# Seven products for queries and keys, PSUM sums and byte masks in a two-layer graph network on one core

## The chip, the cores and the metric

The kernel runs on one core of one Trainium2 chip. The metric is the time of one execution on the device in microseconds (us), here the median over runs.

## The reference

There are 64 graphs of 256 nodes with 256 features (x is 64x256x256, float32) and an adjacency matrix adj (64x256x256, int32, entries 0 or 1, the diagonal set). Each graph passes through two layers. Cut to what matters:

```python
# layer 0: two graph attentions, a norm, a feed-forward block with relu, a norm
def gat(h, W, a):
    Wh = h @ W
    e = leaky_relu(Wh @ a[:256] + swap(Wh @ a[256:]), 0.2)
    return softmax(where(adj > 0, e, -9e15), axis=1) @ Wh
h = norm(x + gat(gat(x, W1, a1), W2, a2), g_ln1, b_ln1)
x = norm(h + relu(h @ w_ff1 + b_ff1) @ w_ff2 + b_ff2, g_ln2, b_ln2)
# layer 1: attention of 8 heads of 32, one value projection for each relation r
q, k = x @ Wq + bq, x @ Wk + bk
attn = softmax(q @ k.T / sqrt(32))
out = sum((attn * (adj == r)) @ (x @ Wv[r] + bv[r]) for r in range(4))
y = norm(x + out @ Wo + bo, g1, beta1)
y = norm(y + gelu(y @ W1 + b1) @ W2 + b2, g2, beta2)
```

## The kernel before

Everything is float32. A graph's 256x256 arrays lie in SBUF as two tiles of 128 partitions. The function `binary` handles adjacency of zeros and ones, for which only relations 0 and 1 occur; a second function, for other adjacency, stands behind a branch that the given data do not take.

The work of a graph is cut into named pieces. `G.` is graph attention up to the first norm, `F.` the first feed-forward block with its norm and then queries and keys, `A.` the attention of layer 1, `T.` the output projection, the second feed-forward block and the last norm, `L.` the loads, `S.` the preparation of weights. Three written lists give the order: `START`, then `PERIOD` for each period, then `END`. An entry `F.q/2` in `PERIOD` runs piece `F.q` for the graph that entered two periods ago, so that six graphs are under way at once. Every engine (PE, DVE, ACT, POOL, and SP, whose queue issues the transfers) executes its own instructions in the order of the lists, and waits at the head of its queue when something it needs is not there. With lags of up to 5 there are 59 full periods.

The pieces that the change and the prediction speak of, and their lines in the code before:

- `G.wh`, `G.wc` project x with the joint weights wx (L751, L761). `G.e` spreads one column of scores into a PSUM tile (L767), `G.lr` adds the other on ACT into the SBUF tile s (L775), `G.ad` on DVE applies the leaky slope (L780), the mask `away` (L781) and takes the maximum (L783), and `G.ex` on ACT takes the exponentials (L788). `G.rz` scales by the inverse sums (L798). `G.gA` and `G.gB` multiply on PE (L804).
- A norm (`ln`, `rs`, `nm`): `ln` on DVE adds the residual to the PSUM result and writes an SBUF tile acc (L506), and takes statistics (L511 to L514); `rs` on POOL takes the root (L518); `nm` on DVE writes the normalised y (L523). `ra`, `rb` on POOL weight y for the next residual (L558, L565). Three norms of a graph have this form; the last one (`D`) has its own finish (L533, L540).
- Turning: `dt` transposes by a DMA in 16-bit words into a tile `pairs` (L473), `dm` moves it by two DMAs into `halves` (L481), and `c` or `mg` joins the halves into float32 on ACT or POOL (L488). Each head of the attention is turned like this, and each y.
- Seven products: `seven_products` replaces the eight block products of a 2x2 block multiplication by seven, with factors and sums prepared (`s` on POOL, L588). Its PE pieces are `a` to `e`; `k1` to `k4` take a first value out of a PSUM bank and `p1` to `p3` add a bank to it (L641). Both first products of the feed-forward blocks (`h`), the second of layer 1 (`f`) and the values (`v`, L852) use it.
- `F.q` and `F.k` are plain products (L839), of two row blocks by two column blocks, and `F.qe`, `F.ke` take them out on ACT with bias and scale (L849). `A.sc` computes the scores of four heads (L884), `A.mx` their maxima, `A.ex` the exponentials, `A.pm` the part with relation 1 (L949), `A.o` the outputs (L957), `A.oc` scales them, and `T.wo` projects (L974).

All PSUM tiles of the loop have one tag with eight buffers, one for each bank; `mm_tile` takes a buffer that is free:

```python
def mm_tile(name, shape=(P, 2, 256)):
    return psum.tile(list(shape), F32, tag="mm", name=name, bufs=8)
```

The joint weights wx are prepared once at the start (`joint_weights`, L341 to L366): W1 times W2 on PE, and both layers' score vectors multiplied in on DVE.

Of the kernel before, what the change touches and what calls it, by code (L numbers as in the profile page):

```python
# [25 lines left out]
F32 = mybir.dt.float32  # L26
U8 = mybir.dt.uint8
# [7 lines left out]
P = 128  # L35
# [8 lines left out]
A.dm10/4 A.mg10/4 L.xT/0 A.zj/4 T.hp2/5 T.ge0/5 A.pm02/4 T.he/5 F.dmA/1 A.pm10/4 F.lnB/2 A.sc0/3  # L44
A.o0/4 T.raC/5 F.cA/1 A.mx10/3 A.o1/4 A.mx03/3 A.mx00/3 T.ge1/5 F.rsB/2 A.oc0/4 A.mx01/3 T.hk4/5
A.dt13/3 A.dt12/3 F.sA/1 T.rbC/5 G.wh0/0 T.ge2/5 L.adj/0 A.oc1/4 T.ge3/5 A.dm13/3 A.ex00/3
A.dm12/3 A.ex01/3 G.wh1/0 G.wc0/0 G.away/0 A.mg12/3 G.wc1/0 F.ha/1 G.eA/0 F.hb/1 A.dt11/3 T.u0/5
A.mx02/3 A.mg13/3 F.nmB/2 G.lrA/0 F.hk1/1 F.hk2/1 T.wo/4 A.ex03/3 A.dt00/3 G.adA/0 T.lnC/4
A.ex10/3 F.raB/3 G.exA/0 A.dm11/3 T.u1/5 A.dm00/3 T.fb/5 A.mg00/3 F.hc/1 T.fa/5 F.hk3/1 A.mg11/3
F.hd/1 G.rzA/0 A.dt03/3 F.hp3/1 F.dtB/2 A.ex02/3 T.fk1/5 F.hp1/1 G.gA0/0 T.rsC/4 G.gA1/0 G.wd0/0  # L50
T.nmC/4 A.dm03/3 G.wd1/0 T.fk2/5 A.va/3 F.dmB/2 T.fp1/5 A.vk1/3 A.vb/3 F.hp2/1 T.dtC/4 G.eB/0
T.u3/5 G.lrB/0 F.rbB/3 T.fc/5 A.iz/3 F.he/1 F.cB/2 A.mg03/3 A.vk2/3 T.fk3/5 T.u2/5 G.adB/0 F.raA/1
A.vc/3 T.fd/5 A.vp1/3 A.dt01/3 F.r0/1 L.x/0 T.fp2/5 G.exB/0 T.dmC/4 A.pm11/3 F.k/2 A.vk3/3 F.q/2
T.fe/5 F.hk4/1 A.zt/3 G.rzB/0 A.pm00/3 A.dm01/3 F.ke0/2 T.cC/4 F.ke1/2 F.r1/1 A.vd/3 A.vp3/3
F.r2/1 F.qe0/2 F.rbA/1 T.fp3/5 A.dt02/3 T.sC/4 T.fk4/5 A.zd/3 A.dt10/3 T.lnD/5 G.gB/0 F.qe1/2
# [9 lines left out]
L.adj:2 L.adj:1 G.wh0:0 S.lr:0 G.away:0 G.wc0:0 G.wh1:0 G.wc1:0 G.eA:0 G.lrA:0 S.f0:0 S.v0:0  # L65
G.adA:0 G.exA:0 G.rzA:0 G.gA0:0 G.gA1:0 G.wd0:0 G.wd1:0 L.xT:1 G.eB:0 G.lrB:0 S.f1:0 G.adB:0
G.exB:0 G.wh0:1 G.wc0:1 S.q0:0 S.j2:0 G.rzB:0 G.wh1:1 G.gB:0 G.wc1:1 S.v1:0 G.away:1 G.eA:1
G.lnA:0 G.lrA:1 S.lw:0 G.rsA:0 L.x:1 G.nmA:0 G.adA:1 S.l0:0 L.xT:2 G.wh1:2 G.exA:1 S.v2:0 G.wh0:2
G.rzA:1 F.raA:0 F.dtA:0 G.wc0:2 L.adj:3 G.gA1:1 S.f2:0 S.q1:0 F.dmA:0 F.cA:0 G.gA0:1 G.wd0:1
F.sA:0 G.wd1:1 F.ha:0 F.hb:0 G.eB:1 S.l1:0 F.hk1:0 F.hk2:0 G.lrB:1 G.wc1:2 F.hc:0 F.hk3:0 G.adB:1  # L70
F.hp3:0 F.hd:0 F.hp2:0 G.exB:1 G.rzB:1 L.xT:3 F.hp1:0 G.wh1:3 F.he:0 F.r0:0 G.gB:1 F.r1:0 F.hk4:0
S.j1:0 F.r2:0 F.r3:0 G.lnA:1 G.away:2 G.wh0:3 G.rsA:1 G.wc0:3 L.x:2 G.nmA:1 G.eA:2 F.f0:0 F.f1:0
G.lrA:2 G.adA:2 F.dtA:1 G.exA:2 F.dmA:1 F.cA:1 G.wc1:3 F.rbA:0 G.rzA:2 S.v3:0 F.lnB:0 S.w1:0
G.gA1:2 G.gA0:2 F.rsB:0 F.ha:1 F.nmB:0 G.eA:3 G.wd0:2 G.wd1:2 G.eB:2 F.hk1:1 F.sA:1 F.hb:1 F.hk2:1
G.lrB:2 F.hc:1 F.hk3:1 L.xT:4 G.adB:2 F.dtB:0 F.dmB:0 F.cB:0 G.away:3 G.exB:2 F.hd:1 F.q:0 F.hp2:1
S.w2:0 F.qe0:0 G.rzB:2 F.qe1:0 F.k:0 F.hp3:1 G.gB:2 F.r0:1 F.ke0:0 F.ke1:0 F.r1:1 A.sc1:0 F.hp1:1
G.lnA:2 G.lrA:3 A.mx12:0 F.he:1 F.hk4:1 A.sc0:0 A.ex12:0 G.rsA:2 F.r2:1 G.nmA:2 F.r3:1 F.sB:0
A.mx13:0 F.raA:1 A.dt12:0 F.dtA:2 A.mx11:0 A.ex11:0 A.mx03:0 A.ex13:0 A.dm12:0 G.adA:3 A.mx01:0
F.dmA:2 F.f0:1 G.exA:3 A.mx10:0 A.dt13:0 A.mx00:0 G.rzA:3 F.rbA:1 A.mg12:0 F.f1:1 A.ex00:0
A.dt00:0 F.cA:2 G.gA1:3 F.sA:2 F.lnB:1 A.dm13:0 F.ha:2 A.ex03:0 F.hb:2 A.mx02:0 A.dm00:0 G.gA0:3  # L80
F.rsB:1 F.hk1:2 F.hk2:2 A.mg00:0 F.nmB:1 F.dtB:1 F.raB:0 G.wd0:3 G.wd1:3 G.eB:3 A.ex10:0 A.dt11:0
G.lrB:3 A.pm12:0 F.hc:2 G.wh0:4 A.mg13:0 G.wh1:4 A.vb:0 F.hk3:2 F.hp1:2 G.adB:3 F.dmB:1 A.dm11:0
F.hd:2 F.raA:2 A.ex02:0 A.va:0 G.wc0:4 F.cB:1 A.dt03:0 F.hp2:2 A.mg11:0 F.raB:1 F.q:1 G.exB:3
A.dt10:0 F.hp3:2 F.rbA:2 F.he:2 G.rzB:3 F.r0:2 A.vk1:0 G.wc1:4 A.ex01:0 A.vk2:0 F.k:1 A.vc:0
F.ke0:1 L.x:3 F.ke1:1 A.dm03:0 A.vk3:0 A.dm10:0 G.gB:3 A.vp3:0 F.qe0:1 A.iz:0 A.mg10:0 A.mg03:0
G.eA:4 F.qe1:1 F.hk4:2 A.pm13:0 G.lnA:3 A.dt02:0 A.pm00:0 A.dt01:0 A.sc1:1 A.mx12:1 A.mx13:1
F.r1:2 F.r2:2 F.r3:2 A.zt:0 A.dm02:0 G.rsA:3 G.nmA:3 A.dm01:0 A.vd:0 G.lrA:4 A.mx11:1 A.pm03:0
A.zd:0 A.ex12:1 A.mg02:0 F.dtA:3 A.ex11:1 A.vp2:0 A.mg01:0 A.pm11:0 A.vp1:0 A.dt12:1 A.zr:0 F.f0:2
A.pm01:0 A.sc0:1 A.pm02:0 A.pm10:0 A.mx01:1 A.ex13:1 F.f1:2 A.dm12:1 A.ve:0 A.mx02:1 A.mx00:1
A.mx10:1 L.adj:4 A.vk4:0 F.lnB:2 A.ex01:1 F.dmA:3 F.rsB:2 A.o1:0 A.mg12:1 G.away:4 F.cA:3 G.adA:4  # L90
# [1248 lines left out]
```

## Time and profile before

| What | Value |
|---|---|
| Median of 3 runs | 3160.0 us (3155.21 to 3164.05) |
| The profiled execution | 3154.81 us, its span 3153.0 us |
| Mean granted TensorE clock | 0.988 |
| PE, DVE, ACT, POOL busy | 95%, 83%, 77%, 59% of the span |

The busy share of PE counts matmuls that overlap one another once, and a matmul that is issued but waits inside the pipeline as busy. A float32 matmul leaves two MATMUL records and two LDWEIGHTS records. In answers about a line, three durations with slashes are the least, the median and the greatest in ns. In answers about a stretch, each engine's busy time stands with the count of its instructions, in the order PE, weight load, DVE, ACT, POOL, then the granted clock, the share of the DMA engines and GB/s. In answers about waits, the total in us, the times and the longest follow the colon. In a timeline, a line has start, length, engine, code line and operation; in brackets stands the idle time before it and what ended it.

### The profile page before, as it was taken

To read this page: it belongs to the slowest core of one execution; us is meant where nothing else is said; L and a number is where in the kernel's file an instruction comes from. 1 tells how busy PE (TensorE), PEld (TensorE's weight loads), DVE (VectorE), ACT (ScalarE), POOL (GpSimd) and SP (SyncE) were. 2 spreads that over 40 slices of the span, in tenths; PEclk is the share of its full clock that TensorE was granted. 3 is DMA by queue.
4 is the path that set the end of the run, shared out by engine and by line. 5 is a ranking of instruction groups with operands and counts; after the bars stand their busy time and mean duration, and the time that the engine had idled before them with its cause. 6 is when DMAs were issued, how large, how long until landed. Compare 5 with 4: busy or idle time off the path is not lost.

```text
span 3153.0 us, 67189 instructions
## 1 busy us (share of the span) xinstructions
PE 3008.8 (95%) x23274; PEld 2615.6 (83%) x23274; DVE 2627.9 (83%) x5425; ACT 2424.5 (77%) x5632; POOL 1861.0 (59%) x2161
## 2 busy tenths in 40 slices
PE   6899999999999999999999999999999999999986
PEld 5688888888888888888888888888888888888875
DVE  5688888898889898888888888888888988888865
ACT  2677877877877877877877877878877877877863
POOL 4466556656656656656556556656656656656554
PEclk8999999999999999999999999999999999999998
DMA  5577777777777787777887777777787777777763
GB/s 162 114 145 152 155 151 148 158 156 149 154 152 149 154 152 145 156 155 149 151 152 153 152 152 152 152 157 152 152 152 150 155 148 151 153 155 148 145 138 69
DMA packets 1049529, 468.72 MB, mean 149 GB/s; under 512 B 788416, under 2 KB 1039296, under 8 KB 1049184
## 3 DMA queue, kind: packets, MB, share of 16 engines
q1 hardware_dynamic: 1047920, 462.12, 73.7%
q8 instruction: 186, 3.05, 0.5%
q0 software_dynamic: 976, 1.72, 0.3%
q14 instruction: 159, 1.30, 0.2%
q10 hardware_dynamic: 288, 0.52, 0.1%
HBM read 75.65 MB, written 17.30 MB: 29 GB/s over the span
## 4 chain that ended last, share of the span: by engine, by line
PE 53%; DMA 15%; DVE 14%; ACT 7%; POOL 4%; issue 4%; SPq 2%; POOLq 0%; DVEq 0%; ACTq 0%
DMA halves_p<-pairs_p 9%; PE ff_a L690 8%; PE fX_c L706 5%; PE hX_c L665 5%; PE o L957 4%; PE hX_a L665 3%; PE q L839 3%; PE k L839 3%; DVE y_c L523 3%; PE gat_b L804 3%; POOL pm L488 3%; PE sc L884 3%; PE wh L751 2%; DMA pairs_p<-p 2%; PE hY_c L665 2%
## 5 line engine op out<-in xcount | busy, mean ns | idle before, releaser
L488 POOL COPY pm<-halves_p 128x1024 uint16<-128x1024 uint16 x256 | 350.5, 1369 | 551.5 <-DMA halves_p<-pairs_p 518.2
L690 PE MATMUL ff_a<-w_L_gnn_w_ff,hid_a 128*128 128x256 f32 x2048 | 463.2, 379 | 0.3 <-ACT hid_a L682 0.3
L949 DVE TENSOR_TENSOR pm<-pm,adj 128x512 f32<-128x512 f32 x512 | 389.6, 794 | 49.9 <-POOL pm L488 48.4
L690 PEld LDWEIGHTS ff_a<-w_L_gnn_w_ff,hid_a 128*128 128x128 f32 x2048 | 379.5, 190 | 48.0 <-issue 0.7
L488 ACT COPY pm<-halves_p 128x1024 uint16<-128x1024 uint16 x256 | 347.0, 1355 | 9.7 <-DMA halves_p<-pairs_p 9.4
L588 POOL TENSOR_TENSOR S_c<-cols_c 128x128 f32<-128x128 f32 x128 | 58.4, 456 | 416.0 <-ACT cols_c L488 416.0
L957 PE MATMUL o<-pm,v 128*32 128x256 f32 x4096 | 236.7, 381 | 4.3 <-POOL pm L488 1.7
L682 ACT ACTIVATE hid_c<-hid_c,col_L_gnn_b 128x256 f32<-128x256 f32 x512 | 224.5, 498 | 4.9 <-DVE hid_c L641 2.0
L682 ACT ACTIVATE hid_a<-hid_a,col_L_gnn_b_ff 128x256 f32<-128x256 f32 x512 | 223.9, 501 | 0.7 <-DVE hid_a L641 0.6
L957 PEld LDWEIGHTS o<-pm,v 128*32 128x32 f32 x4096 | 126.2, 110 | 104.1 <-issue 21.8
L706 PE MATMUL fX_c<-f_L_gnn_W,hid_c 128*128 128x128 f32 x1536 | 205.0, 276 | 3.3 <-ACT hid_c L682 2.4
L706 PEld LDWEIGHTS fX_c<-f_L_gnn_W,hid_c 128*128 128x128 f32 x1536 | 197.0, 192 | 12.2 <-ACT hid_c L682 3.6
L523 DVE TENSOR_SCALAR y_c<-acc_c,mv_c,rstd_c 128x256 f32<-128x256 f32 x128 | 157.2, 1268 | 34.4 <-POOL rstd_c L518 34.4
L488 ACT COPY cols_a<-halves_y_a 128x1024 uint16<-128x1024 uint16 x64 | 86.4, 1349 | 101.5 <-DMA halves_y_a<-pairs_y_a 101.3
L884 PE MATMUL sc<-kT,qT 32*128 32x256 f32 x2048 | 148.9, 400 | 0.9 <-DVE v L641 0.9
L665 PEld LDWEIGHTS hX_c<-S_c,f_L_gnn_W 128*128 128x128 f32 x1024 | 128.9, 191 | 24.0 <-issue 20.2
L665 PEld LDWEIGHTS hX_c<-cols_c,f_L_gnn_W 128*128 128x128 f32 x1024 | 134.3, 192 | 14.2 <-ACT cols_c L488 4.8
L665 PE MATMUL hX_a<-cols_a,f_L_gnn_w_ff 128*128 128x128 f32 x1024 | 137.6, 277 | 6.0 <-ACT cols_a L488 2.9
L775 ACT ACTIVATE s_B<-e_B,wh_B 128x256 f32<-128x256 f32 x128 | 53.7, 471 | 116.4 <-PE e_B L767 116.4
L852 PE MATMUL vY<-f_Wv,S_y 128*128 128x256 f32 x256 | 84.4, 412 | 61.2 <-DVE acc_c L641 57.9
L665 PEld LDWEIGHTS hX_a<-cols_a,f_L_gnn_w_ff 128*128 128x128 f32 x1024 | 128.6, 192 | 16.8 <-ACT p L899 8.0
L665 PE MATMUL hX_c<-cols_c,f_L_gnn_W 128*128 128x128 f32 x1024 | 136.5, 276 | 5.4 <-ACT cols_c L488 3.6
(1741 smaller groups left out, 9328.8 us busy)
## 6 DMA issues: line engine op xcount, KB each, us to landing
halves_p<-pairs_p SPq DMA_DIRECT2D x1024, 128.0 KB, 3.3
xT<-in_xT SPq DMA_DIRECT2D x64, 256.0 KB, 3.5
adj<-in_adjT SPq DMA_DIRECT2D x64, 256.0 KB, 3.3
x<-in_x SPq DMA_DIRECT2D x64, 256.0 KB, 3.3
halves_y_a<-pairs_y_a SPq DMA_DIRECT2D x128, 128.0 KB, 3.9
halves_y_y<-pairs_y_y SPq DMA_DIRECT2D x128, 128.0 KB, 3.3
zs<-flat SPq DMA_DIRECT2D x256, 64.0 KB, 2.7
halves_y_c<-pairs_y_c SPq DMA_DIRECT2D x128, 128.0 KB, 3.2
```

The lines of the kernel that those rows point to most:

```text
L488: copy(into().bitcast(U16).rearrange("p (n s) -> p s n", s=2), t["halves"].rearrange("p s k q -> p s (k q)"),)
L523: nc.vector.tensor_scalar(y[:, :, :, i, :], tiles["acc"][:, i, :].rearrange("p (k c d) -> p c k d", k=KC, c=2), tiles["mv"][:, i, 0:1], ti ...
L665: nc.tensor.matmul(ps[:, f * P : (f + 1) * P], weights()[0][:, factor, f * P : (f + 1) * P], left, start=start and f == 0, stop=f == FC // ...
L682: nc.scalar.activation(tiles["hid"][:, f, :], tiles["hid"][:, f, :], func, bias=b1[:, f : f + 1])
L690: nc.tensor.matmul(tiles["ff"][:, i, :], tiles["hid"][:, f, nodes(i)], weights()[2][:, f, :], start=(f == 0), stop=(f == FC - 1),)
L706: nc.tensor.matmul(ps, left[:, f, :], weights()[2][:, factor, f * P : (f + 1) * P], start=start and f == 0, stop=f == FC // 2 - 1, skip_gr ...
L804: nc.tensor.matmul(ps, t["s"][:, j, nodes(i)], t["whz"][:, j, :width], start=(j == 0), stop=(j == NT - 1),)
L839: nc.tensor.matmul(t[key + "p"][:, o, :], w[:, c, nodes(o)], tiles["cols"][:, c, :], start=(c == 0), stop=(c == KC - 1),)
L852: nc.tensor.matmul(ps, left, wv[:, factor, :], start=start, stop=True, skip_group_check=True)
L884: nc.tensor.matmul(t["sc", g, hh][:, i, :], qkv["q"][hd, g, nodes(i)], qkv["k"][hd, g, :], start=True, stop=True,)
L949: nc.vector.tensor_tensor(pm[:, 1, :], pm[:, 0, :], tiles["adj"], ALU.mult)
L957: nc.tensor.matmul(ps[hh * DH : (hh + 1) * DH, :], qkv["v"][:, j, d0 : d0 + DH], t["pm", (g, hh)][:, r, j * N : (j + 1) * N], start=(r == ...
```

## The change

1. **Queries and keys.** Wq and Wk become one set of seven factors `wqk`, prepared like those of the values, with the biases in one tile `bqk`; the query half is scaled by 1/sqrt(32) in the preparation. Pieces `F.q`, `F.k`, `F.qe0/1`, `F.ke0/1` go; `F.qa` to `F.qe`, `F.qk1` to `F.qk4` and `F.qp1` to `F.qp3` come. The first values are taken out on DVE with the bias added.
2. **PSUM.** A norm adds the residual in place in the PSUM bank, and statistics and y read the bank. The scores of the graph attention after slope and mask are written to the bank of `e`, and the exponentials read it.
3. **Bytes.** `A.pm` takes the mask as bytes from `away`, which therefore lives as long as the graph's attention (four buffers), while the int32 adjacency has one buffer instead of four.
4. **Buffers.** `pairs` and `halves` have three tiles instead of two, `pm` seven instead of eight.
5. **Joint weights.** The part of W1 comes before that of the product W1 W2; W1 is loaded on ACT's queue; the score sums are written straight into wx.
6. **Orders.** `START`, `PERIOD` and `END` are new throughout.

```diff
-T.nmC/4 A.dm03/3 G.wd1/0 T.fk2/5 A.va/3 F.dmB/2 T.fp1/5 A.vk1/3 A.vb/3 F.hp2/1 T.dtC/4 G.eB/0
+A.ex03/3 F.lnB/2 G.wc0/0 A.oc0/4 F.dmA/1 A.va/3 A.oc1/4 A.ex01/3 G.wh1/0 T.u0/5 A.mg13/3 F.rsB/2
+A.vb/3 G.away/0 A.dt12/3 F.nmB/2 A.vk1/3 G.wc1/0 A.vk2/3 F.raA/1 T.wo/4 T.u1/5 G.eA/0 F.cA/1
...
+F.hp3/1 G.wd0/0 T.fp1/5 F.qa/2 A.pm13/3 T.dmC/4 F.hp2/1 T.u2/5 F.qb/2 T.fc/5 A.zd/3 A.dt00/3
...
+T.fe/5 F.hk4/1 G.adB/0 F.r1/1 F.qe/2 T.fk4/5 G.exB/0 F.qk4/2 T.lnD/5 T.ha/4 T.sC/4 T.hk1/4 F.rbA/1
+T.nmD/5 G.rzB/0 T.hb/4 T.rsD/5 A.sc1/2 A.mx10/2 A.pm03/3 T.hk2/4 A.dm00/3 T.rbC/4 T.hp1/4 A.o1/3
...
-        for a, n in ((a2, "L0_gnn_a2"), (a1, "L0_gnn_a1")):
+        for a, n in ((a1, "L0_gnn_a1"), (a2, "L0_gnn_a2")):
...
-        for w, n in ((w1T, "L0_gnn_W1T"), (w2, "L0_gnn_W2"), (w1, "L0_gnn_W1")):
-            nc.sync.dma_start(out=w, in_=t[n].rearrange("(c p) n -> p c n", p=P))
+        for queue, w, n in (
+            (nc.sync, w1T, "L0_gnn_W1T"), (nc.scalar, w1, "L0_gnn_W1"), (nc.sync, w2, "L0_gnn_W2"),
+        ):
+            queue.dma_start(out=w, in_=t[n].rearrange("(c p) n -> p c n", p=P))
...
-        nc.vector.tensor_copy(wx[:, :, :D], ps)
-        for w, a, at in ((wx, a2, SRC2), (w1, a1, SRC1)):
+        for w, a, at in ((w1, a1, SRC1), (wx, a2, SRC2)):
+            if w is wx:
+                nc.vector.tensor_copy(wx[:, :, :D], ps)
             for c in range(KC):
-                both = small.tile([P, 2], F32, tag="wa", name=f"wa_{at}_{c}", bufs=1)
                 prod = work.tile([P, 2, D], F32, tag="res", name=f"prod_{at}_{c}", bufs=3)
-                nc.vector.tensor_tensor(
-                    prod, a, w[:, c, :D].unsqueeze(1).to_broadcast([P, 2, D]), ALU.mult
-                )
-                nc.vector.tensor_reduce(both, prod, AX.X, ALU.add)
-                nc.vector.tensor_copy(wx[:, c, at : at + 1], both[:, 1:2])
-                nc.vector.tensor_copy(wx[:, c, at + 1 : at + 2], both[:, 0:1])
+                for half in range(2):
+                    nc.vector.tensor_tensor(prod[:, half, :], a[:, 1 - half, :], w[:, c, :D], ALU.mult)
+                nc.vector.tensor_reduce(wx[:, c, at : at + 2], prod, AX.X, ALU.add)
...
-            t["pairs"] = work.tile([P, 2, 4, P], U16, tag="pairs", name=f"pairs_{name}", bufs=2)
+            t["pairs"] = work.tile([P, 2, 4, P], U16, tag="pairs", name=f"pairs_{name}", bufs=3)
...
-            acc, *terms = src()
-            if terms:
-                acc = work.tile([P, NT, D], F32, tag="acc", name=f"acc_{name}", bufs=2)
-                nc.vector.tensor_tensor(acc, *terms, ALU.add)
+            acc, *residual = src()
+            if residual:
+                nc.vector.tensor_tensor(acc, acc, *residual, ALU.add)
...
-            ps = t["e"] = mm_tile(f"e_{step}{b}", (P, N))
+            t["e"] = mm_tile(f"e_{step}{b}", (P, NT, N))
...
-            nc.vector.scalar_tensor_tensor(t["s"], t["s"], ALPHA, t["s"], ALU.mult, ALU.max)
-            nc.vector.scalar_tensor_tensor(t["s"], t["away"], NEG, t["s"], ALU.mult, ALU.add)
+            nc.vector.scalar_tensor_tensor(t["e"], t["s"], ALPHA, t["s"], ALU.mult, ALU.max)
+            away = tiles["away"].rearrange("p (t i) -> p t i", t=NT)
+            nc.vector.scalar_tensor_tensor(t["e"], away, NEG, t["e"], ALU.mult, ALU.add)
...
-        def project(w, key):
-            t[key + "p"] = mm_tile(f"{key}_{b}")
+        def columns(ps, factor, left, start):
             for o in range(KC):
-                for c in range(KC):
-                    nc.tensor.matmul(
-                        t[key + "p"][:, o, :], w[:, c, nodes(o)], tiles["cols"][:, c, :],
-                        start=(c == 0), stop=(c == KC - 1),
-                    )
...
+                nc.tensor.matmul(
+                    ps[:, nodes(o)], wqk[:, factor, nodes(o)], left,
+                    start=start and o == 0, stop=o == KC - 1, skip_group_check=True,
+                )
...
+        def begin_qk(i, h, ps):
+            nc.vector.tensor_tensor(
+                qk(i, h), ps.rearrange("p (o n) -> p o n", n=P),
+                bqk[:, h, :].unsqueeze(2).to_broadcast([P, KC, P]), ALU.add,
+            )
...
+        seven_products(do, "F", "q", b, *by_columns(tiles), columns, begin_qk, qk, D)
...
-            nc.vector.tensor_tensor(pm[:, 1, :], pm[:, 0, :], tiles["adj"], ALU.mult)
+            nc.vector.scalar_tensor_tensor(
+                pm[:, 1, :], tiles["away"], 0.0, pm[:, 0, :], ALU.is_equal, ALU.mult
+            )
```

## The prediction

> **What bounds the kernel now.** I read the busy rows first, then the same counts in four windows far from both ends, then the waits of PE and SP, then a piece of PE's timeline, and last the rows of the DVE lines that the change touches.
>
> ```profile
> PE 3008.8 (95%) x23274; PEld 2615.6 (83%) x23274; DVE 2627.9 (83%) x5425; ACT 2424.5 (77%) x5632; POOL 1861.0 (59%) x2161
> ```
> ```profile
> 540.00:1015.00 475.00, 465.31 (x3651) 406.60 (x3650) 410.60 (x847) 381.30 (x888) 289.27 (x334) 1.00 0.76 153
> sum 1900.00, PE 1855.26 PEld 1621.87 DVE 1632.86 ACT 1520.73 POOL 1149.25; mean PE 463.81 PEld 405.47 DVE 408.21 ACT 380.18 POOL 287.31
> ```
> ```profile
> PE vY L852 <- DVE acc_c L641: 57.9, 57, 1.9
> PE wh L751 <- DVE wx L366: 9.0, 1, 9.0
> SPq L473 <- DMA halves_p<-pairs_p: 343.9, 410, 2.8
> ```
> ```profile
> 1540.07 1.06 PE L665 MATMUL hX_a<-cols_a,f_L_gnn_w_ff 128*128 128x128 f32 x8
> 1540.96 0.60 PE L852 MATMUL vX<-f_Wv,S_y 128*128 128x256 f32 x2
> ...
> 1542.72 1.89 PE L839 MATMUL k<-cols_y,w_L_gnn_Wk 128*128 128x256 f32 x8
> 1544.45 1.89 PE L839 MATMUL q<-cols_y,w_L_gnn_Wq 128*128 128x256 f32 x8
> 1546.18 1.05 PE L706 MATMUL fX_c<-f_L_gnn_W,hid_c 128*128 128x128 f32 x8
> ...
> 1584.98 0.70 PE L852 MATMUL vY<-f_Wv,S_y 128*128 128x256 f32 x2 [1.25 <-DVE acc_c L641]
> ...
> 1587.52 1.06 PE L665 MATMUL hX_a<-cols_a,f_L_gnn_w_ff 128*128 128x128 f32 x8
> ```
> ```profile
> L523 DVE TENSOR_SCALAR y_a<-acc_a,mv_a,rstd_a x128: 402/544/1347, 45.0 to 2972.8; 128x256 f32<-128x256 f32 x128
> L523 DVE TENSOR_SCALAR y_c<-acc_c,mv_c,rstd_c x128: 399/1352/1422, 164.5 to 3114.8; 128x256 f32<-128x256 f32 x128
> L949 DVE TENSOR_TENSOR pm<-pm,adj x512: 628/684/1807, 112.6 to 3103.0; 128x512 f32<-128x512 f32 x171
> L781 DVE SCALAR_TENSOR_TENSOR s_B<-away,s_B x64: 691/1647/1661, 36.6 to 2959.4; 128x512 f32<-128x512 uint8 x64
> L506 DVE TENSOR_TENSOR acc_a<-gat_b,x x64: 686/691/693, 42.0 to 2968.5; 128x512 f32<-128x512 f32 x64
> ```
>
> The same hX_a group starts at 1540.07 and 1587.52: a period is 47.45 us, and 1900 us hold 40 of them. In a period PE is busy 1855.3/40 = 46.4 us and idle 1.1; DVE works 40.8, ACT 38.0, POOL 28.7. PE is the bound. About 1.0 of its 1.1 us of idling is one wait, 57 times in the run: bank Y of the value products waits for a DVE add that empties a bank of the last feed-forward product (`A.vb` stands two entries behind `T.fp1` in the written order). So only two things can shorten the middle: fewer matmul columns, and that wait. Beside it PE idles 353 - 278.8 = 74 us in the first 200 and last 153 us.
>
> **Queries and keys by seven products.** From 1542.72 to 1546.18, k and q take 3.46 us: 16 records of 256 columns, 0.216 each (a matmul leaves two records). The new form has seven products of two matmuls: 28 records of 128 columns. The nearest rows are hX_a and fX_c, also 128x128 by 128 columns, eight per group: 1540.07 to 1540.96 is 0.89, or 0.111 each. 28 x 0.111 = 3.12 us, so -0.34 per graph. Here the Trainium skill speaks against the change: "TensorE: Matmul & The Clock Gate", section "Back-to-back issue gap", gives a sustained 81 ns for a 128-column matmul because its weight load must be paid too. With two passes per record that would be 28 x 0.162 = 4.5 us, +1.1 per graph, +69 us in all. The row has loads and products together at 0.111, so I take the row. A group that really waited starts slower (a vY pair 0.53 after its wait, to 1585.51, against 0.44 at 1540.96); there are now five pieces instead of two, and I allow one such start, +0.11. Net -0.23.
> Off PE: ACT loses four evictions of 0.465, -1.9 us. DVE gains four first sums and three adds over 128x256 from PSUM, 7 x 0.415 (the v rows of L641 and L866) = +2.9. POOL gains nothing, for the sums S_y exist already for v; but `F.qb` now waits for them on POOL's queue (4 x 0.53), where queries formerly needed only the columns, and the scores behind it wait for seven DVE pieces rather than four ACT ones. If these are late, `A.sc1` stops PE, with everything queued behind it. The cover is three 0.89 us groups, `T.ha` and `T.hb`, between the last piece `F.qk4` and `A.sc1`: 2.7 us, for a DVE piece of 0.415 and what is queued ahead of it.
>
> **Norm sums and graph scores in PSUM.** The sums, statistics and y now read PSUM. y costs 1.268, 0.793 and 0.550 us in the mean, twice each, 5.2 per graph, though each form can take 0.4. "SBUF — State Buffer", section "Terms", says that DVE and GpSimd lock a shared port pair and the loser blocks for a whole instruction; a y of 1352 against 399 is about one POOL instruction (1.15 for the weighted residual) longer. Against the change stands "VectorE: DVE Perf Modes", section "Why PSUM operands drop a tier": one PSUM source costs an fp32 operation its double rate. By that rule y should be dearer from PSUM; but no y row goes below 0.396, so there is no double rate here to lose. Statistics and reductions have the same price from either memory (row L783 0.686, the score maxima 0.68). I take 6 x 0.41 = 2.5: -2.8 us. L781 keeps one SBUF input: from 1.416 + 1.209 to 2 x 0.69, -1.2; L780 keeps two and stays. L506 writes PSUM instead of SBUF, taken as equal (bounds -0.1 and +0.1 each, as row-to-row scatter).
> This is DVE time, hidden under PE. What it costs is banks: `gat_b`, `ff_a` and `wo` are held from their sum on through statistics (1.36 us), the root on POOL (0.75, plus up to 1.4 for what POOL is doing) and y (0.8), some 2.9 us longer, three times a period, and e until the exponentials. The queries' third bank comes on top. All eight banks are shared.
>
> **Masking by bytes.** Eight DVE products per graph, 0.76 to 0.79 each, become scalar_tensor_tensor with a byte operand. Nearest: L781's undisturbed 0.691 against 0.628 to 0.684. Two SBUF inputs remain. Bounds -0.3 and +0.8 per graph; I take +0.3. Adjacency now has one buffer: its load waits for the previous `G.away`, which the new order places most of a period earlier; 3.3 us to land is covered.
>
> **Three tiles of pairs and halves; seven pm.** SP waits 343.9 us for halves before it may issue the next transpose, and POOL's joins idle 518 us for landings. A third tile loosens this; PE waits only 1.7 us for those joins, so it is worth nothing directly. Bounds 0 and -5 us. When the buffer is no longer last, the transfer itself is: DMA share is already 0.76. Losing the eighth pm tile delays joins on ACT and POOL until `A.o` has run; PE has over 6 us of work between each reuse and that release along the list. Nothing.
> DVE per period: 40.8 + 2.9 - 2.8 - 1.2 + 0.3 = 40.0; ACT 36.1. Both stay below PE.
>
> **Joint weights, start and end.** `wh` waits 9.0 us for wx. Today DVE idles to 11.67, then does the copy and four blocks in series, until 21.5. Now W1 follows a1 and a2 on ACT's queue, landing near 8.8 (issue about 1.7, 7.1 to land); its two blocks (3.0 us) fit before the copy, and two remain after it: ready near 15.6. -6 on graph 0's chain; the 20 us thereafter have DMA at 0.99, so I take -5 (bounds -8 and +3). Of the other start and end entries I can only say that the 74 us of idle time bound them; I take 0, bounds -15 and +15.
>
> **New orders.** In the new list `A.va`, `A.vb` stand well ahead of `T.fp1`; their banks can come from `A.oc0`, `A.oc1` and the graph copies. The present wait loses its cause. But `F.qa` now stands directly behind `T.fp1`, and `A.o0` has one free bank. I count 0.82 of the 1.0 us as gained and leave 0.2 for what is late next.
>
> **The sum.** Middle: -0.23 - 0.82 = -1.05, to 46.4; 59 full periods, -62. Five more graphs at -0.23, -1. Start -5. The profiled execution took 3154.8 (span 3153.0): 3087. The median of 3160.0 lies 5 above that execution, so 3092.
>
> **Rivals.**
> (A) As summed: 3092; its own range 3055 to 3125. For it: DVE and ACT have slack and the wait has one named cause. Chance 0.57.
> (B) The wait moves. `F.qa` takes the bank that `T.fp1` has just freed, exactly as vY did, or the scores wait for the last query piece. Then 64 x 0.23 + 5 = 20 us remain: 3140. For it: vY took the newest freed bank although others were free. Chance 0.27.
> (C) Slower: banks held through the norms stop PE. If the 2.9 us hits one group in every second period, that is +1.45 against -1.05: 59 x 0.40 - 6 = +18, 3178; in every period, 3263. It decides from 1.15 us of new waiting per period. Against it: the old list had three places with a single free bank, the new one has one. Chance 0.12.
> (D) The narrow products cost what the skill's rule says: 3154.8 + 69 - 48 - 5 + 5 = 3176. The rows speak against it. Chance 0.04.
>
> **How the numbers follow.** About 0.3%, 9.5 us, is what a measurement of this kernel can tell from no change. Faster: A and four fifths of B, 0.78. Same: 0.08, from B's upper end and C's lower. Slower: 0.14, from C and D. The range 3050 to 3160 leaves out most of C and D and a little of A.
>
> **What would show it.** Right: q and k near 3.1 us; a period near 46.4; no vY wait; y near 0.41; DVE near 40 us a period; wh starting near 15 us. Wrong: a PE wait of a microsecond each period, on `qX`, `sc`, or a bank whose releaser is y or an exponential (B, C), or 128-column query records at 0.16 (D).

## The result and the profile after

| | Before | After |
|---|---|---|
| Median | 3161.56 us (3155.21 to 3164.56, 6 runs) | 3148.28 us (3143.82 to 3151.91, 6 runs) |
| Profiled execution, span | 3153.0 us | 3145.9 us |
| Ratio, 95% interval | | 0.9957 (0.9944 to 0.9971) |

The change gains 13 us where 68 had been forecast. The direction was right and the size was not. The middle of the run, where the forecast had placed 62 us, gained nothing. The mean distance from one `gat_b` to the next over 50 periods was 47.25 us before and is 47.39 now, which is 8 us lost over 59 periods. The gain lies at the end. In the profiled executions, from the start of the 56th `wo` to the last instruction it takes 382.6 us instead of 396.9, while the sixth `wo` starts 2.0 us later than before (394.5 against 392.5). The forecast had put the end at nothing, so that the direction came out right was luck.

The busy row and the chain of waits of the profile after, and then the chain of the profile before:

```profile
PE 3017.6 (96%) x24042; PEld 2623.3 (83%) x24042; DVE 2793.8 (89%) x5870; ACT 2323.2 (74%) x5374; POOL 1887.4 (60%) x2165
...
DVE 36%; PE 31%; DMA 15%; ACT 6%; issue 4%; SPq 4%; POOL 2%; ACTq 0%; DVEq 0%; POOLq 0%
DVE whz_B L810 5%; PE ff_a L699 5%; DMA halves_p<-pairs_p 5%; DMA halves_y_c<-pairs_y_c 4%; DVE hid_c L650 3%; DMA halves_y_a<-pairs_y_a 3%; SPq L490 3%; PE o L973 3%; PE wh L760 2%; PE wo L990 2%; PE hX_c L674 2%; PE sc L898 2%; PE fX_c L715 2%; PE gat_a L816 2%; DVE e_A L791 2%
```
```profile
PE 53%; DMA 15%; DVE 14%; ACT 7%; POOL 4%; issue 4%; SPq 2%; POOLq 0%; DVEq 0%; ACTq 0%
```

DVE's busy time has risen from 2627.9 to 2793.8 us, and the chain that ended last now runs more through DVE (36% against 14% before) than through PE. Its first line is a small scaling, `whz_B`, that the forecast did not mention.

The same four windows as before, summed, and then what PE waited for, both of the kernel after:

```profile
sum 1900.00, PE 1864.29 PEld 1625.74 DVE 1742.55 ACT 1459.74 POOL 1164.17; mean PE 466.07 PEld 406.43 DVE 435.64 ACT 364.94 POOL 291.04
```
```profile
PE gat_b L816 <- DVE pm L963: 17.1, 15, 1.6
PE hX_a L674 <- ACT cols_a L497: 17.0, 15, 4.3
PE w L357 <- DMA in_w<-in_L_gnn_W: 14.4, 1, 14.4
PE gat_b L816 <- ACT p L913: 12.7, 24, 1.6
PE vX L868 <- DVE v L650: 12.5, 35, 0.6
```

In 1900 us DVE now works 1742.55 us instead of 1632.86. By the period that is 43.5 us; the forecast was 40.0. The old wait of vY is gone from the list, and several smaller ones stand in its place. Their sizes in a period come from the starts of the matmul records, as what the distance from one start to the next exceeds the usual one: 0.65 us ahead of `gat_b`, 0.30 ahead of vX, 0.27 ahead of hX_c and 0.19 ahead of hX_a, together 1.4. (The list of waits gives less, since part of such a distance counts as busy.)

Of the seven products for queries and keys, the first three in a row, of four records each:

```profile
1552.35 0.61 PE L850 MATMUL qX<-cols_y,f_Wqk 128*128 128x128 f32 x4
1552.80 0.61 PE L850 MATMUL qZ<-cols_y,f_Wqk 128*128 128x128 f32 x4
1553.24 0.61 PE L850 MATMUL qY<-S_y,f_Wqk 128*128 128x128 f32 x4
```

The DVE rows that answer to those of before, with `whz_B` in the kernel after and, last, in the kernel before:

```profile
L532 DVE TENSOR_SCALAR y_a<-gat_b,mv_a,rstd_a x128: 533/536/545, 47.3 to 2990.0; 128x256 f32<-128x256 f32 x128
L532 DVE TENSOR_SCALAR y_c<-wo,mv_c,rstd_c x128: 533/535/545, 167.4 to 3107.5; 128x256 f32<-128x256 f32 x128
L963 DVE SCALAR_TENSOR_TENSOR pm<-away,pm x512: 674/746/1793, 127.1 to 3098.6; 128x512 f32<-128x512 uint8 x171
L810 DVE TENSOR_SCALAR whz_B<-wh_B,grz_B x128: 342/1444/1485, 40.1 to 2981.0; 128x256 f32<-128x256 f32 x128
L798 DVE TENSOR_SCALAR whz_B<-wh_B,grz_B x128: 348/352/356, 39.5 to 2964.0; 128x256 f32<-128x256 f32 x128
```

The y rows no longer spread: from PSUM they are never over 545 ns, where y_c had a median of 1352. But `whz_B`, which never took more than 356 ns before, now has a median of 1444. A piece of the timeline shows why, and who is behind it:

```profile
1564.23 2.80 DVE L810 TENSOR_SCALAR whz_B<-wh_B,grz_B 128x256 f32<-128x256 f32 x2
1564.26 1.28 POOL L574 TENSOR_TENSOR res_c<-res_c,row_L_gnn_beta 128x512 f32<-128x512 f32 x1
1565.48 2.74 POOL L497 COPY pm<-halves_p 128x1024 uint16<-128x1024 uint16 x2
...
1566.95 0.67 DVE L905 TENSOR_REDUCE am_(1, 0)_17670<-sc 128x2 f32<-128x512 f32 x1
...
1567.66 0.47 ACT L913 ACTIVATE p<-sc,am_(1, 0)_17670 128x256 f32<-128x256 f32 x1 [2.76 <-DVE am_(1, 0)_17670 L905]
...
1568.73 0.94 PEld L816 LDWEIGHTS gat_b<-whz_B,s_B 128*128 128x128 f32 x5 [1.00 <-ACT p L913]
1568.73 1.13 PE L816 MATMUL gat_b<-whz_B,s_B 128*128 128x256 f32 x4 [0.81 <-DVE pm L963]
```

Two scalings that need 0.35 us each take 2.80 us: each is held up by the POOL instruction beside it (1.28, then a join of 1.37). Behind them on DVE's queue stands the maximum of a head's scores, behind that on ACT the exponentials of that head, which ACT waits 2.76 us to begin, and these release the PSUM bank that `gat_b` takes. `gat_b` starts when they have ended, after a wait of 0.81 us. One row names the exponentials `p` as the releaser and one the mask product of L963, which ended at about the same time. The records decide between them: from the sixth graph on, all 59 starts of `gat_b` come 52 or 53 ns after the last instruction of these exponentials has ended, and in two of the periods in which it waited the mask product had ended 13 us or more earlier.

The records also say who holds the scalings up. Of the 128 in the run, 121 took over 0.7 us, and each of these ended 146 to 155 ns after a POOL instruction had ended. In the kernel before, no POOL instruction ran beside any of the 128. And 195 of the 384 y from PSUM had a POOL instruction beside them for over 0.1 us; all took 527 to 545 ns.

### The profile page after: what moved, and what is told of

The parts are those of the page before. It is cut to its first block, busy times and chain, and to the rows that moved or that the text cites. A ratio compares the mean times of both kernels' runs of the same rounds, so it can differ in the third digit from the quotient of the medians.

```text
span 3145.9 us, 69222 instructions
## 1 busy us (share of the span) xinstructions
PE 3017.6 (96%) x24042; PEld 2623.3 (83%) x24042; DVE 2793.8 (89%) x5870; ACT 2323.2 (74%) x5374; POOL 1887.4 (60%) x2165
## 4 chain that ended last, share of the span: by engine, by line
DVE 36%; PE 31%; DMA 15%; ACT 6%; issue 4%; SPq 4%; POOL 2%; ACTq 0%; DVEq 0%; POOLq 0%
DVE whz_B L810 5%; PE ff_a L699 5%; DMA halves_p<-pairs_p 5%; DMA halves_y_c<-pairs_y_c 4%; DVE hid_c L650 3%; DMA halves_y_a<-pairs_y_a 3%; SPq L490 3%; PE o L973 3%; PE wh L760 2%; PE wo L990 2%; PE hX_c L674 2%; PE sc L898 2%; PE fX_c L715 2%; PE gat_a L816 2%; DVE e_A L791 2%
## 5 line engine op out<-in xcount | busy, mean ns | idle before, releaser
L963 DVE SCALAR_TENSOR_TENSOR pm<-away,pm 128x512 f32<-128x512 uint8 x512 | 456.2, 901 | 10.6 <-ACT pm L497 6.2
L527 POOL TENSOR_TENSOR rstd_a<-var_a,neghalf 128x2 f32<-128x2 f32 x64 | 44.9, 702 | 411.7 <-DVE var_a L523 411.7
L973 PE MATMUL o<-pm,v 128*32 128x256 f32 x4096 | 248.4, 382 | 0.9 <-DVE pm L963 0.7
L691 ACT ACTIVATE hid_a<-hid_a,col_L_gnn_b_ff 128x256 f32<-128x256 f32 x512 | 231.6, 507 | 3.7 <-DVE hid_a L650 3.7
L597 POOL TENSOR_TENSOR S_c<-cols_c 128x128 f32<-128x128 f32 x128 | 79.7, 623 | 207.1 <-ACT cols_c L497 207.1
L597 POOL TENSOR_TENSOR S_y<-cols_y 128x128 f32<-128x128 f32 x128 | 85.1, 665 | 154.1 <-ACT cols_y L497 132.4
L810 DVE TENSOR_SCALAR whz_B<-wh_B,grz_B 128x256 f32<-128x256 f32 x128 | 171.7, 1381 | 2.3
L816 PE MATMUL gat_b<-whz_B,s_B 128*128 128x256 f32 x512 | 129.1, 395 | 33.0 <-DVE pm L963 17.1
L674 PEld LDWEIGHTS hX_c<-cols_c,f_L_gnn_W 128*128 128x128 f32 x1024 | 125.1, 192 | 34.9 <-DVE hid_c L650 30.4
L898 PE MATMUL sc<-qk 32*128 32x256 f32 x2048 | 149.1, 404 | 0.0
```

The costliest lines, as they stand in the source:

```text
L597: engine.tensor_tensor(to[i], one, other, op)
L674: nc.tensor.matmul(ps[:, f * P : (f + 1) * P], weights()[0][:, factor, f * P : (f + 1) * P], left, start=start and f == 0, stop=f == FC // ...
L691: nc.scalar.activation(tiles["hid"][:, f, :], tiles["hid"][:, f, :], func, bias=b1[:, f : f + 1])
L810: nc.vector.tensor_scalar_mul(t["whz"][:, j, :width], t["wh", step][:, j, :width], rz[:, j : j + 1])
L816: nc.tensor.matmul(ps, t["s"][:, j, nodes(i)], t["whz"][:, j, :width], start=(j == 0), stop=(j == NT - 1),)
L898: nc.tensor.matmul(t["sc", g, hh][:, i, :], qkv["q"][hd, g, nodes(i)], qkv["k"][hd, g, :], start=True, stop=True,)
```

## The experiments

The theory was this: **the change did not remove DVE's collisions with POOL but moved them**, from y, behind which little stood, to `whz_B`, behind which stand the score maxima and in the end PE. Summed over all DVE lines, what exceeds a line's quick form comes to some 6.5 us a graph before and 5.7 after. The rivals: held banks (the prediction's case C), the seven products' load on DVE, and DVE's load as such.

**whz of step B on ACT.** One instruction is taken out of POOL's reach.

```diff
             for j in range(NT):
+                if step == "B":
+                    nc.scalar.activation(
+                        t["whz"][:, j, :width], t["wh", step][:, j, :width], AF.Copy,
+                        scale=rz[:, j : j + 1],
+                    )
+                    continue
```

> The changed kernel, with the scaling of whz in step B (two 128x256 products) on ACT instead of DVE; the reciprocal stays on DVE. Theory 1 (the port contention moved to whz_B, 1.38 us each instead of 0.35; it delays the score maxima behind it on DVE, these the exponentials, and these the bank that gat_b needs): the 0.65 us per period in front of gat_b goes, DVE falls from 43.5 to about 40.7 us per period, and the time falls by some 38 us, to about 3110. Theory 2 (banks held through the norms stop PE whatever DVE does): DVE falls as much, but the waits of PE stay and the time stays within 10 us of 3148. Theory 3 (the DVE work of the seven products' evictions makes DVE late): in between, a gain of 10 to 25 us.

Measured: 3076.82 us, ratio to before 0.9725 (0.9709 to 0.9742); against the change's 0.9957 that is 73 us. Its scaling, its windows, and its first PE wait:

```profile
L811 ACT ACTIVATE whz_B<-wh_B,grz_B x128: 492/507/540, 41.3 to 2921.7; 128x256 f32<-128x256 f32 x128
```
```profile
sum 1900.00, PE 1885.46 PEld 1662.49 DVE 1682.32 ACT 1519.66 POOL 1202.44; mean PE 471.37 PEld 415.62 DVE 420.58 ACT 379.92 POOL 300.61
```
```profile
PE vX L874 <- DVE v L650: 16.0, 49, 0.6
```

The period is 46.33 us, where the prediction had 46.4. The gap ahead of `gat_b` falls from 0.65 to 0.06, those ahead of hX_c and hX_a from 0.46 together to under 0.07; only that ahead of vX grows, from 0.30 to 0.41. So the prediction's own time for the middle was there to be had, and this instruction stood in its way. The norms' sums stay in PSUM here, and the banks with them. The gain was about twice what the waits ahead of `gat_b` alone had let me expect, for the waits ahead of hX_c and hX_a went too.

**The same edit in the kernel before.**

> The kernel before with one edit: the scaling whz of step B runs on ACT (0.50 us each) instead of DVE. In the trace of the kernel before this scaling takes 0.348 to 0.356 us, never more, so POOL does not hold it up there. Theory 1 (the 73 us gained by the same edit in the changed kernel come from POOL's contention, which the new order put on this scaling): nothing to gain here; 2 x 0.35 us less DVE work that lies beside PE and 1.0 us more ACT, so 3160 +- 8 us, ratio 0.998 to 1.003. Theory 2 (DVE's load as such sets the period, and any 2 x 0.35 us off it helps): 20 to 40 us faster, ratio near 0.990.

Measured: ratio 1.0012 (0.9998 to 1.0025). The edit is worth nothing where POOL leaves the scaling alone (352 ns there), though it takes DVE work away there too. That alone speaks of the old order only. But across all runs the time does not follow DVE's load either: DVE works 1574 us in the windows of 1900 us in a run of 3154 us (the norms alone, below), 1595 in one of 3203 (plain products on ACT), and 1699 in one of 3055 (the last below).

**The collision moved by one entry of the order.** whz stays on DVE.

```diff
-T.nmD/5 G.rzB/0 T.hb/4 T.rsD/5 A.sc1/2 A.mx10/2 A.pm03/3
+G.rzB/0 T.hb/4 T.rsD/5 A.sc1/2 A.mx10/2 T.nmD/5 A.pm03/3
```

> The changed kernel with one entry of the order moved: T.nmD/5 (two DVE instructions of 0.49 us) stands behind A.mx10/2 instead of in front of G.rzB/0, so that whz of step B starts on DVE about 0.9 us earlier, while POOL takes its small root instead of a residual and a join. Nothing else moves, whz stays on DVE. Theory 1 (POOL's instruction holds whz up, and only that): whz falls from 1.38 to under 0.6 us, the maxima and the exponentials come 1.5 to 2 us earlier, PE's wait ahead of gat_b goes: 3075 to 3095. Theory 2 (what helped when whz ran on ACT was the smaller load of DVE, not the collision): 3140 to 3150. Theory 3 (the collision passes on to T.nmD's instructions or to the masking and the maxima are as late as before): whz fast, but 3120 to 3150.

Measured: 3156.07 us, ratio 0.9982 (0.9970 to 0.9993); the third theory, with nothing at all gained. From its DVE rows (the second with busy us and mean ns), its timeline and its PE waits:

```profile
L810 DVE TENSOR_SCALAR whz_B<-wh_B,grz_B x128: 341/352/1353, 41.2 to 2988.4; 128x256 f32<-128x256 f32 x128
L542 DVE SCALAR_TENSOR_TENSOR res_d<-acc_c,mv_d,row_L_gnn_g 128x256 f32<-128x256 f32 x128 | 149.5, 1206 | 1.3 <-DMA out<-res_d 1.3
```
```profile
1565.68 0.62 DVE L810 TENSOR_SCALAR whz_B<-wh_B,grz_B 128x256 f32<-128x256 f32 x2
...
1567.55 2.79 POOL L497 COPY pm<-halves_p 128x1024 uint16<-128x1024 uint16 x2
1567.61 2.95 DVE L542 SCALAR_TENSOR_TENSOR res_d<-acc_c,mv_d,row_L_gnn_g 128x256 f32<-128x256 f32 x2
```
```profile
PE hX_c L674 <- DVE hid_c L650: 59.6, 59, 2.1
```

whz is back at 352 ns, and the maximum starts 1.16 us after the first product of the scores (the median), against 3.55 in the changed kernel. But the same two POOL joins now meet `res_d`, which rises from 0.497 to 1.206 us in the mean. Behind it on DVE stands the add that empties a bank for hX_c, and PE waits for that 59 times, 1.0 us each. The period is 47.48 us: the wait had a new address and about the same size. With whz on ACT, the maximum also starts after 1.16 us; but there what has moved up beside the same POOL work is the maximum itself, which reads PSUM and takes 0.69 us beside POOL's weighted residual. So it is the collision that counts, and what stands behind the instruction that is hit.

**The norms in PSUM alone**, in the old order: the residual is added in place, all else as before.

> The kernel before with one part of the change: the three norms add their residual in place in the PSUM bank and read statistics and y from it; all else, the order too, as before. Theory 1 (the sources of y in PSUM are out of POOL's way: 0.53 us each as in the changed kernel, against 1.27, 0.79 and 0.55 in the mean): DVE 2 us a period less, but beside PE; and the banks held some 3 us longer cost little, as in the changed kernel: 3150 to 3170. Theory 2 (the contention moves to the next DVE instruction with SBUF operands, as it did to whz): y falls, but other lines (pm, whz, the slope of the scores) rise by about what y gains, DVE's sum stays near 40.8 us a period. Theory 3 (rival C of the prediction: held banks stop PE in the old order, which has three places with one free bank): 3200 or more.

Measured: 3154.06 us, ratio 0.9988 (0.9975 to 1.0000). Three of its rows, by shape (busy, mean ns), its first PE wait, and a piece of the timeline at that wait:

```profile
L780 DVE SCALAR_TENSOR_TENSOR s_B<-s_B 128x512 f32<-128x512 f32 x64 | 83.5, 1305 | 14.1 <-ACT s_B L775 11.3 <-PE wh L751 2.7
...
L523 DVE TENSOR_SCALAR y_c<-wo,mv_c,rstd_c 128x256 f32<-128x256 f32 x128 | 63.2, 533 | 3.7 <-POOL rstd_c L518 3.7
...
L781 DVE SCALAR_TENSOR_TENSOR s_B<-away,s_B 128x512 f32<-128x512 uint8 x64 | 55.2, 863 | 2.2
```
```profile
PE sc L884 <- ACT v L868: 39.5, 59, 0.7
```
```profile
1554.58 0.71 PE L884 MATMUL sc<-kT,qT 32*128 32x256 f32 x6
...
1555.54 0.36 ACT L868 COPY v<-vX 128x256 f32<-128x256 f32 x1
...
1555.95 1.13 PE L884 MATMUL sc<-kT,qT 32*128 32x256 f32 x10 [0.67 <-ACT v L868]
```

Two things follow. First, keeping the norms' sums in PSUM costs no time in the sum of the run, even in the order with three places of a single free bank. It is not without a wait: vY's wait is gone, and instead the scores stop after three heads' banks, until an ACT copy has emptied the bank of vX, 59 times, 0.67 us each. That is a wait for a bank, of the kind that case C feared, at less than half of C's 1.45 us a period; whether the held banks are its cause was not tested. Second, y's collisions did not pass to `whz_B` here (0.359 in the mean, 0.352 before): so what put them there is the new order, or something that came with it, not the norms alone. In step B the collision only changed lines: the slope L780 rises from 0.712 to 1.305, the mask L781 falls from 1.416 to 0.863. DVE's sum fell (1574.39 us in 1900, from 1632.86), and the period stayed at 47.31.

**The graph scores back in SBUF**, in the changed kernel (slope, mask, maximum and exponentials on `s`).

> The changed kernel, with the scores of the graph attention kept in SBUF as before (slope, mask, maximum and exponentials on s), so that the bank of e is free after the two ACT pieces. Theory 1 and 3: the masking line blocks again, up to 1.2 to 1.6 us instead of 0.70, DVE gets 1 to 1.9 us per period more, and the time rises by 10 to 50 us. Theory 2: two banks are free earlier, and the time falls by 5 to 30 us.

Measured: 3188.72 us, ratio 1.0077 (1.0057 to 1.0098), 38 us slower than the change. The mask of step A then costs 1.031 us instead of 0.696, and the gaps ahead of `gat_b` and vX grow to 0.79 and 0.59. An earlier release of e's bank gains nothing here, and the lines that grow are those that now have all their operands in SBUF.

**Plain products for queries and keys**, in three forms. First in the changed kernel, with the two products taken out on ACT as before the change:

```diff
-        seven_products(do, "F", "q", b, *by_columns(tiles), columns, begin_qk, qk, D)
+        do["F.qa"], do["F.qd"] = partial(project, 1), partial(project, 0)
+        do["F.qk1"], do["F.qk2"] = partial(keep_qk, 1, 0), partial(keep_qk, 1, 1)
+        do["F.qp2"], do["F.qk4"] = partial(keep_qk, 0, 0), partial(keep_qk, 0, 1)
```

> The changed kernel, with queries and keys as plain products of 256 columns, taken out by ACT in four pieces with the bias, at places of the seven pieces in the same order. PE gets 0.33 us per period more, DVE 2.9 us less. Theory 1: whz_B stays blocked and gat_b still waits, so the time rises by 5 to 20 us, to 3155 to 3170. Theory 2: about +21 us, for only the columns count. Theory 3: the late DVE was due to these pieces; the waits of PE go, -0.65 - 0.3 + 0.33 per period, and the time falls by 20 to 40 us.

Measured: 3203.28 us, ratio 1.0119 (1.0102 to 1.0137), outside every expectation. The wait ahead of `gat_b` had gone, but whz still took 1.45 us in the median, and a wait of the experiment's own had come:

```profile
PE e_B L776 <- ACT wh_B L770: 29.9, 60, 0.5
```

The four ACT evictions stand in the order ahead of the copies of wh that `e_B` needs. The run therefore said nothing on the products. Next, with whz on ACT besides:

> The changed kernel with whz of step B on ACT (3076.8 us so far) and, besides, queries and keys as two plain products again, taken out on ACT; the seven products' pieces are empty. Theory 1: with the contention out of the way the seven products are worth their PE time alone, 0.33 us for each of 64 graphs, so 3077 + 21 = 3098. Theory 2 (the seven products cost DVE seven adds, 2.9 us a graph, and what PE still waits, 0.42 us a period on a value taken out by DVE, is theirs): without them the wait goes too, 3077 + 21 - 25 = 3073, no slower. Theory 3 (ACT's queue: the four evictions stand ahead of the copies of wh, as in the run with plain products, where PE waited 0.98 us a period on e of step B): 3098 + 59 = 3157.

Measured: 3166.49 us, ratio 1.0017 (1.0005 to 1.0030). The wait on wh stayed (30.3 us in the list, and 0.98 us a period in the records), as the third theory had it. Last, with the evictions as four DVE adds:

```diff
-            nc.scalar.activation(
-                t["qk"[h]][:, o, :], t["ps", h][:, o, :], AF.Identity, bias=bqk[:, h, o : o + 1]
-            )
+            nc.vector.tensor_tensor(
+                t["qk"[h]][:, o, :], t["ps", h][:, o, :],
+                bqk[:, h, o : o + 1].to_broadcast([P, N]), ALU.add,
+            )
```

> The changed kernel with whz of step B on ACT (3076.8 us), and queries and keys as two plain products, taken out with their bias by four DVE adds of 0.42 us instead of four ACT evictions. Taken out on ACT they gave 3166, with PE waiting 0.98 us a period for ACT's copy of wh ahead of e of step B. Theory 1 (that wait is ACT's queue, not PE's columns): without the evictions on ACT the wait is gone and what is left is the PE time of the products alone, 0.33 us x 64 = 21: 3098. Theory 2 (DVE's seven adds are a cost of the seven products, so that three fewer of them, 1.2 us a graph, shorten PE's other wait on DVE): 3077 + 21 - 20 = 3078. Theory 3 (the plain products disturb the written order itself): 3150 or more.

Measured: 3110.22 us, ratio 0.9846 (0.9828 to 0.9864), against 0.9725 with seven products: they are worth 38 us, with both intervals 27 to 49. 0.33 us of PE for 64 graphs make 21 of that; the period, 46.71 against 46.33, makes 22, and the rest lies at the ends or within the interval. The first theory was nearest. Three adds fewer on DVE brought nothing (second theory), since PE does not wait for them.

**Masking by bytes alone**, in the old order.

> The kernel before with the masking by bytes alone (away with four buffers, adjacency with three). In the changed kernel the masking takes 0.90 us in the mean against 0.79, minimum 0.674 against 0.628. Theory 1 (the form itself costs 0.05 us undisturbed, and the rest of the rise came from the new order's collisions with POOL): about 0.84 in the mean, +0.4 us of DVE a period beside PE, 3160 to 3170. Theory 2 (the rise of 0.11 each is the byte form's own, and DVE's delays reach PE's wait on vY): 0.90, +0.9 us of DVE a period, 3175 to 3200.

Measured: ratio 1.0003 (0.9987 to 1.0019). The byte form has a minimum of 628 ns and a mean of 785, against 628 and 794 before. It is free. In the changed kernel the mean is 901: that rise is not the byte form's.

**A third tile of halves**, with the bytes and two adjacency buffers fewer, in the old order.

> The kernel before with the masking by bytes (worth nothing by itself: 1.0003 of before) and, with the room that two fewer adjacency buffers leave, a third tile of halves; pairs stay at two, pm at eight. In the kernel before, SP's queue waits 343.9 us for halves before it may issue the next transposes, but PE waits 1.7 us in all for the joins behind them. Theory 1 (the prediction's: the third tile loosens SP and shortens nothing that PE waits for): 0 to -5 us, 3155 to 3162. Theory 2 (the joins on POOL and ACT come earlier[...], so that vY's wait changes): 15 us or more in either direction.

Measured: 3154.62 us, ratio 0.9983 (0.9969 to 0.9997), within the prediction's 0 to -5 us. SP's wait for halves was 350.7 us, against 343.9, so one tile more of halves alone does not loosen SP's queue. The third tile of pairs and the loss of the eighth pm were not measured alone, and neither were the new lists. Norm sums in SBUF and int32 masks were not tried under the new order.

**The joint weights alone**, in the old order.

> The kernel before with the new preparation of the joint weights alone (W1 on ACT's queue, its part first, sums written straight into wx). Prediction: wx about 6 us earlier, the time 5 us less (3156, ratio 0.998). Rival: the first graph's chain is bound by other loads, and the time is unchanged within 2 us; or W1 lands late behind a1 and a2 and the time rises by up to 3 us.

Measured: 3170.02 us, ratio 1.0022 (1.0008 to 1.0037), later where 5 us had been forecast to be gained. Its second PE wait:

```profile
PE w L354 <- DMA f_L_gnn_w_ff<-in_L_gnn_w_ff: 16.1, 1, 16.1
```

**W1 back on SP's queue behind W2**, in the changed kernel with whz on ACT; the new order of the two parts is kept.

> The changed kernel with whz of step B on ACT (3076.8 us so far) and W1 loaded on SP's queue behind W2, as before the change, with the new order of the two parts kept. Theory 1 (W1 on ACT's queue takes bandwidth from W2; the product W1 W2 began at 14.4 us instead of 8.2): W2 is back at 8 us, W1 lands near 11.7, then two blocks, the copy and two blocks in series on DVE (some 7 us): wx ready near 19, 2 to 3 us earlier; 3074, ratio to the other about 0.999. Theory 2 (graph 0's chain is bound by what comes after): no change, 3077.

Measured: 3075.91 us, ratio 0.9738 (0.9718 to 0.9757): no difference from 0.9725. From the timeline of its start (the last two lines from a longer stretch):

```profile
8.43 3.75 PE L357 MATMUL w<-in_w,in_w1T 128*128 128x256 f32 x8 [8.43 <-DMA in_w<-in_L_gnn_W]
9.78 1.10 DVE L367 TENSOR_TENSOR prod<-in_a,in_w 128x256 f32<-128x256 f32 x3 [8.90 <-DMA in_w<-in_L_gnn_W]
...
15.16 4.23 PE L760 MATMUL wh<-wx,xT 128*128 128x260 f32 x8 [2.97 <-DVE wx L368]
...
28.53 3.83 PE L760 MATMUL wh<-wx,xT 128*128 128x260 f32 x8 [8.32 <-DMA xT<-in_xT]
32.15 2.62 PE L822 MATMUL gat_a<-whz_A,s_A 128*128 128x258 f32 x8
```

Here wh starts at 15.16 us, the prediction's figure, instead of 20.63. Yet `whz_B` of the first graph starts only 1.3 us earlier than with W1 on ACT's queue (39.97 against 41.30). The trace shows what came between. PE's next product belongs to the second graph, and PE idles 8.32 us until that graph's x has landed, at 28.53 (29.61 with W1 on ACT's queue); SP issues this load at 25.07, behind the weights. `gat_a` of the first graph, whose scaling is done at 25.24, stands behind that product on PE and starts at 32.15.

**A try at the best version:** this kernel with one more entry moved (lines of the list cut, the rest of it only wrapped anew).

```diff
-T.nmC/4 A.vd/3 F.hp1/1 T.dtC/4 T.fa/5 A.mg12/3 A.vp2/3
+T.nmC/4 A.vd/3 A.vp2/3 F.hp1/1 T.dtC/4 T.fa/5 A.mg12/3
```

> A try at the best version: the changed kernel with whz of step B on ACT, W1 back on SP's queue (3075.9 us so far), and A.vp2/3 moved forward to stand directly behind A.vd/3, ahead of F.hp1, T.dtC and T.fa. PE still waits 0.30 us a period on vX for a bank that this DVE add frees, held up behind a 0.68 us add and a slope of 1.8 us. Theory 1: 0.68 us earlier, the wait of 0.30 goes: 59 x 0.30 = 18 us, 3058. Theory 2 (another wait takes its place, hid_a's bank freed 0.41 us later): 3070 to 3080.

Measured: 3054.63 us, ratio to before 0.9668 (0.9649 to 0.9687), faster than both kernels and 22 us below the version without the moved entry (0.9738), near the first theory. Its four windows:

```profile
sum 1900.00, PE 1899.14 PEld 1676.32 DVE 1698.72 ACT 1534.63 POOL 1211.47; mean PE 474.78 PEld 419.08 DVE 424.68 ACT 383.66 POOL 302.87
```

The period is 45.88 us and PE idles 0.86 us in 1900. The mask (917 ns) and the slope of step A (1.620 us) still collide with POOL, but PE waits for neither. By these records PE's own work is all that is left in the middle.

## Why the prediction was right or wrong, point by point

- **The bound, and the one wait.** Right: vY's wait is gone. The base was slightly off: 47.45 us was one pair of starts, the mean of 50 periods is 47.25. The sum is not touched by that, since it counts differences; but 1.05 us less than 47.25 is 46.20, not 46.4, and with whz on ACT 0.92 of the 1.05 was reached.
- **Seven products on PE.** Right: 28 records, of which the twelve shown take 1.34 us from the first start to the next group's at 1553.69, or 0.112 each; that is 3.1 us a graph, as forecast. The Trainium skill's 81 ns for a 128-column matmul ("TensorE: Matmul & The Clock Gate", "Back-to-back issue gap"), taken twice for each record, would by estimate have made 4.5; the row decided well. On DVE, 0.410 to 0.421 each, as forecast. The plain products for comparison gave 38 us where the sum had 15: the 0.11 allowed for a late start was not needed (that makes 21), and the other 17 lie outside the steady periods or within the interval of 27 to 49.
- **y from PSUM: the step that failed first.** The text took 0.41 us and set aside the Trainium skill's rule ("VectorE: DVE Perf Modes", "Why PSUM operands drop a tier") with "there is no double rate here to lose". The trace has 0.535, 0.133 more than the 0.396 to 0.402 of an undisturbed y from SBUF. So there was something to lose, and the rule was right on the sign; why the difference has this size is not shown. It is 6 x 0.12 = +0.7 us of DVE a period, still far less than the collisions that y was rid of.
- **"-2.8 us" of DVE, and "leave 0.2" of waiting: the step that decided.** I counted the collisions removed from y and added no term for where POOL's instructions would strike next. DVE did not fall from 40.8 to 40.0 but rose to 43.5. By row, per period: `whz_B` 2 x 1.03 = +2.06, masking 8 x 0.107 = +0.86, the two slopes +0.44, the products +2.9, against y -2.0 and the mask of the scores -1.2; together +3.0, and the windows show 2.7. On PE, 1.4 us a period of waiting came where 0.2 had been left. The lock that I quoted for y from the Trainium skill ("SBUF — State Buffer", "Terms") struck `whz_B` and `res_d` in the same way, so it had to be carried through the new order.
- **"DVE time, hidden under PE": wrong.** The sum of DVE is under PE's, but a piece of it is not free when something stands behind it in the queue. Taking `whz_B` with its extra 2.1 us a period off DVE gained 73 us in the run, because the maxima, the exponentials and a bank of `gat_b` come after it.
- **Banks held (C).** C did not happen. In the old order the norms in PSUM exchanged one wait of PE for another and cost nothing in the sum; in the changed kernel most of PE's waiting went when `whz_B` moved, with all banks held as before. I had asked to look for a bank released by an exponential as the mark of C; the mark appeared, but the exponential was late, the bank was not held for long.
- **Rival B, "the wait moves",** was nearest in size (3140), with the wrong place: neither `F.qa` nor the scores, but `gat_b`.
- **Bytes, halves and statistics:** costs near nothing, as forecast (the statistics take 0.411 from SBUF and 0.416 from PSUM). Only the rise of the byte mask to 0.90 was not theirs. The loss of the eighth pm was not measured alone.
- **Start.** Wrong by its own step: W1 was forecast to land near 8.8 beside the others, but its transfer put W2 off, and `w` began at 14.4 instead of 8.2. wh started at 20.63 instead of 15. With W2 first, 15.16 was reached, and it gained little: PE's queue then waited for the second graph's x, so the 5 us were not on the path either.
- **The sum.** Middle: -62 forecast, +8 measured. That is the missing 70 us, and the waits account for about all of it: 1.4 us a period where 0.2 were left is 1.2 x 59 = 71. The end gave about -14 in the profiled executions, near the edge of the 15 that I allowed it; which entry of `END` brought it was not taken apart.

## What to carry to other kernels

When a change frees an instruction from a collision with another engine, do not book the time as saved: go through the new order and name the instruction that now stands beside the same POOL work, and what is queued behind it. Look for the line whose minimum is unchanged but whose median has jumped; of all lines that collide, the one to take off the engine is the one from which a chain of short waits leads to the bounding engine. Moving it to another place in the order only helps if what takes its place cannot be stopped.

## What the runs showed of the hardware

- A DVE scaling of 0.35 us from and to SBUF can take about the whole of the POOL instruction beside it (2.80 us for two, beside 1.28 and 1.37); the 121 slow ones ended 146 to 155 ns after a POOL instruction. Not every POOL instruction does this: with the entry moved, 118 such scalings ran beside POOL's small root (128x2, about 0.70 us) and took 346 to 355 ns.
- The same kind of instruction with its source in PSUM stayed within 0.524 to 0.547 us in the two kernels shown with y from PSUM, though it writes to SBUF, and though POOL worked beside 195 and 376 of the 384.
- Such instructions with two SBUF sources and a per-partition factor (`res_d`) are stopped too: 0.497 against 1.206 us in the mean.
- A mask of bytes costs a two-source DVE operation nothing against an int32 mask (minimum 628 ns for both in the old order). In the changed kernel its minimum was 674, but so it was for the int32 mask in the old order with the norms in PSUM; why is open.
- Two weight loads on separate queues at the start went with a later landing of the first needed: the product of both began at 14.4 us, and at 8.4 with both loads on one queue, the needed one first.
